# Newton step and softplus correction with one operand in PSUM, and a new placing of the stages, in a pair of Mamba scans

## The chip, the cores and the metric

The kernel runs on one core of a Trainium2 chip, as one launch that takes the whole input from HBM and leaves the whole output there. The metric is the device time of a run in microseconds (us). Three runs of the kernel before took 3250.43, 3251.8 and 3252.24 us; the median is 3251.8 us.

## The reference, cut to what matters

Four layers stand one after another on an image batch x of shape (2, 128, 56, 56), each as `x = x + layer(group_norm(x))`: an attention with agents, a 3x3 convolution, a mixture of eight experts on 2x2 patches, and a pair of Mamba blocks, one that reads each image row forwards and one that reads it backwards. The change touches the last layer alone. All of it is float32.

```python
xc = silu(conv_b + causal_conv(xi))                       # 256 channels, sequences of 56
dt, Bm, Cm = split(xc @ xproj_w.T)                        # rank 8, 16 states, 16 states
dt = softplus(dt @ dt_w.T + dt_b)
A = -exp(Alog)
for each position l:                                      # for each channel and state
    h = exp(dt_l * A) * h + (dt_l * u_l) * B_l
    y_l = sum over states (h * C_l)
y = (y + xc * D) * silu(z);  out = y @ out_w.T
...
y = concat(forward, backward) @ fuse_w.T
y = (y - mean) / sqrt(var + 1e-5) * ln_w + ln_b           # over the 128 channels
x = x + y
```

## The kernel before, in words

`mamba_pair` takes the image in 14 blocks (2 batches of 7) of 448 pixels, which are 8 image rows. Each block has two halves, f (forwards) and b (backwards), and each half has 16 units: 8 pairs of states by 2 halves of the channels. A unit is one scan over 128 partitions by 896 elements. The loop at the end of `mamba_pair` does one unit per step, so a block takes 32 steps, called f0 to f15 and b0 to b15 here, and the layer 448.

In one step the engines do this, in this order of the code. ScalarE (ACT) computes the decay exp(dt A) of the next unit (`decay`, L1648, two ACTIVATEs) into one of two PSUM tiles dA. Then ACT takes results of stages of the step before out of PSUM (`fetch`). GpSimd (POOL) computes dBu of the unit three steps ahead (`push`, L1659) into one of four buffers. VectorE (DVE) scans (`scan`, L1681). After the second scan of a pair of states, at odd units, the pair's h is multiplied by C: by POOL at L1687 for the pairs of states listed in `POOLED`, else by DVE at L1690, with C spread over the partitions by TensorE (PE) in a PSUM bank (`read_out`, L1669). PE adds up y of the unit three steps back (`collect`, L1701), and `close` (L1707, DVE) multiplies a finished y by the gate three steps into the next half.

Everything else that the blocks need is booked on steps with `book(step, stage, tag, late)` and run at the end of that step: what the next block needs before its scans (norm, convolution, silu, the low-rank product, softplus), and what the finished block needs after them (fuse, the norm over channels, turning back, adding onto x). `at` is the block's first step less 32, so that offset 0 to 31 lies in the block before and 32 to 63 in the block itself. A stage that leaves its product in PSUM returns a function that ACT runs one step later, or two with `late=1`. The order so written is the order on every engine[...]. Two single PSUM banks serve these stages: the one tagged "mm", and the one tagged "c" that `read_out` uses also. The rest of PSUM is dA (four banks) and y (two).

The two parts that the change rewrites:

The softplus of dt is log(1 + exp(-|s|)) + relu(s), with a correction. `step` (L1591) makes s on PE, and ACT writes |s| into `sp_e` and relu(s) into `dt`. `exps` (L1605) makes e = exp(-|s|) and u = 1 + e for both halves of the channels, 896 elements at a time, in SBUF. `error` (L1611, DVE) computes (u - 1) - e, what rounding added to u: two inputs, both in SBUF. `log` takes ln u, and `softplus` (L1619) adds the three terms on PE.

The norm over channels works on 112 partitions by 4 values. `measure` takes mean and variance; `root` (L1490, L1491, ACT) makes a first 1/sqrt(var + eps) through Ln and Exp into `ln_rstd` in SBUF; `newton` (L1496 to L1499, DVE) improves it by one Newton step, in three instructions with two SBUF inputs each, and makes the shift with a fourth; `normalize` (L1503, ACT) applies both.

Other names used below: `silu(inputs, gates)` (L1709) loads an activation table, does two Silu ACTIVATEs of 896 elements and loads the first table again; `weigh` (L1624, POOL) makes dt times u for `send_steps`, whose DMAs bring it to the partitions where `push` reads it; `onto` (L1524, POOL) adds the result to x.

Of the kernel before, what the change touches and what calls it, by code (L numbers as in the profile page):

```python
# [8 lines left out]
F32 = mybir.dt.float32  # L9
AF = mybir.ActivationFunctionType  # L10
ALU = mybir.AluOpType
# [6 lines left out]
P = 128  # L18
# [3 lines left out]
BLK = 448  # L22
NBLK = N // BLK
ROWS = BLK // HW
T = 112
NT = BLK // T
# [1264 lines left out]

MAMBA_STATES, MAMBA_RANK, MAMBA_TAPS = 16, 8, 4

POOLED = {"f": (0, 3, 6), "b": (1, 3)}


class MambaWeights:


    def __init__(self, net, one, nat, bank):  # L1300
# [19 lines left out]
        for n, d in enumerate("fb"):  # L1320
# [5 lines left out]
            w.d = d  # L1326
            w.pooled = POOLED[d]

# [57 lines left out]
def mamba_pair(net, out, wts, combine):  # L1386
# [5 lines left out]
    tc, nc, a = net.tc, net.nc, net.a  # L1392
# [13 lines left out]
    with ExitStack() as ctx:  # L1406
        work = ctx.enter_context(tc.tile_pool(name="l3_work", bufs=2))
# [31 lines left out]
        def mm(name):  # L1439
            return ps.tile([P, 512], F32, name=name, tag=place["tag"])  # L1440

        class Block:
# [43 lines left out]

            def root(self):
                t = net.small.tile([T, NT], F32, name="ln_t", tag="ln_t")
                self.rstd = net.small.tile([T, NT], F32, name="ln_rstd", tag="ln_rstd")
                nc.scalar.activation(t, self.mv[:, :, 1], AF.Ln, bias=net.eps[:T])  # L1490
                nc.scalar.activation(self.rstd, t, AF.Exp, scale=-0.5)  # L1491

            def newton(self):
                t = net.small.tile([T, NT], F32, name="ln_t", tag="ln_t")
                self.shift = net.small.tile([T, NT], F32, name="ln_shift", tag="ln_shift")
                nc.vector.scalar_tensor_tensor(t, self.mv[:, :, 1], 1e-5, self.rstd, ALU.add, ALU.mult)  # L1496
                nc.vector.scalar_tensor_tensor(t, t, -0.5, self.rstd, ALU.mult, ALU.mult)  # L1497
                nc.vector.scalar_tensor_tensor(self.rstd, t, 1.5, self.rstd, ALU.add, ALU.mult)  # L1498
                nc.vector.scalar_tensor_tensor(self.shift, self.mv[:, :, 0], -1.0, self.rstd, ALU.mult, ALU.mult)  # L1499

            def normalize(self):
                for t in range(NT):
# [25 lines left out]
        class Half:  # L1528
# [62 lines left out]
            def step(self, m):  # L1591
                pm = mm("dt_ps")
                nc.tensor.matmul(pm[:, :BLK], self.w.dt_t[:, m, :], self.lo[:R, :], start=True, stop=True)
                if m == 0:
                    self.e = work.tile([P, 2, BLK], F32, name="sp_e", tag="sp_e", bufs=1)
                    self.dt = work.tile([P, 2, BLK], F32, name="dt", tag="dt")
                bias = self.w.dt_b[:, m : m + 1]

                def fetch():
                    nc.scalar.activation(self.e[:, m, :], pm[:, :BLK], AF.Abs, bias=bias)  # L1600
                    nc.scalar.activation(self.dt[:, m, :], pm[:, :BLK], AF.Relu, bias=bias)

                return fetch

            def exps(self):  # L1605
                self.u = work.tile([P, 2, BLK], F32, name="sp_u", tag="sp_u", bufs=1)
                nc.scalar.activation(self.e, self.e, AF.Exp, scale=-1.0)
                nc.scalar.activation(self.u, self.e, AF.Identity, bias=1.0)

            def error(self):  # L1610
                nc.vector.scalar_tensor_tensor(self.e, self.u, 1.0, self.e, ALU.subtract, ALU.subtract)  # L1611

            def log(self):
                nc.scalar.activation(self.u, self.u, AF.Ln)  # L1614

            def softplus(self, m):
                pm = mm("sp_ps")
# [91 lines left out]
        def silu(inputs, gates):  # L1709

            if inputs:
                nc.scalar.activation(inputs.xc, inputs.xc, AF.Silu)
            if gates:
                nc.scalar.activation(gates.zs, gates.zs, AF.Silu)
            nc.scalar.preload_act_table_set(EXP_LN)  # L1715

        blocks = [Block(b, k) for b in range(NB) for k in range(NBLK)]
# [3 lines left out]
        def book(step, *stages, tag="mm", late=0):  # L1721

            agenda.setdefault(step, []).extend((stage, tag, late) for stage in stages)

        for n, blk in enumerate(blocks):

            f, b = blk.ways
            at = STEPS * (n - 1)
            if n == 0:
                book(at + 1, blk.norm)  # L1730
                for i, (h, m) in enumerate(((f, 0), (f, 1), (b, 0), (b, 1))):
                    book(at + 4 + 2 * i, lambda h=h, m=m: h.conv(m))
                    book((1, 4, 5, 13)[i], lambda h=h, m=m: h.gate(m))
                book(at + 14, lambda f=f: silu(f, None), lambda b=b: silu(b, None))
                book(at + 16, f.low)
                book(at + 17, f.send_low)
                for h, t in ((f, at + 18), (b, 2)):
                    for m in range(2):
                        book(t + m, lambda h=h, m=m: h.step(m))
                        book(t + 5 + m, lambda h=h, m=m: h.softplus(m))  # L1740
                    book(t + 2, h.exps)
                    book(t + 3, h.error)
                    book(t + 4, h.log)
                book(at + 25, f.weigh)
                book(at + 25, f.send_steps)
                book(0, b.low)
                book(2, b.send_low)
                book(11, b.weigh, b.send_steps)
            else:
                before = blocks[n - 1]  # L1750
                book(at + 4, blk.norm)
                book(at + 7, lambda f=f: f.conv(0), late=1)
                book(at + 9, lambda f=f: f.conv(1), late=1)
                book(at + 11, lambda b=b: b.conv(0), late=1)
                book(at + 11, lambda b=b: b.conv(1), tag="c", late=1)
                book(at + 12, lambda f=f, g=before.ways[0]: silu(f, g))
                book(at + 14, f.low)
                book(at + 16, lambda b=b, g=before.ways[1]: silu(b, g))
                book(at + 17, lambda f=f: f.step(0), tag="c", late=1)
                book(at + 17, lambda f=f: f.step(1), late=1)  # L1760
                book(at + 18, f.send_low)
                book(at + 20, f.exps)
                book(at + 21, f.error)
                book(at + 21, b.low, tag="c")
                book(at + 22, f.log)
                book(at + 22, lambda f=f: f.softplus(0), tag="c")
                book(at + 23, lambda f=f: f.gate(0))
                book(at + 24, lambda f=f: f.softplus(1))
                book(at + 25, lambda b=b: b.step(0), tag="c")
                book(at + 25, lambda b=b: b.step(1))  # L1770
                book(at + 26, f.weigh)
                book(at + 27, f.send_steps)
                book(at + 28, lambda f=f: f.gate(1), late=1)
                book(at + 30, b.exps)
                book(at + 30, b.error)
                book(at + 32, b.log)
                book(at + 32, lambda b=b: b.softplus(0), tag="c")
                book(at + 32, b.send_low)
                book(at + 34, lambda b=b: b.gate(0))
                book(at + 35, lambda b=b: b.softplus(1))  # L1780
                book(at + 38, b.weigh)
                book(at + 39, b.send_steps)
                book(at + 45, lambda b=b: b.gate(1))

            at = STEPS * (n + 1)
            book(at + 4, lambda blk=blk: blk.fuse(0))
            book(at + 4, lambda blk=blk: blk.fuse(1), late=1)
            book(at + 6, blk.measure)
            book(at + 9, blk.root)
            book(at + 10, blk.newton)  # L1790
            book(at + 11, blk.normalize)
            book(at + 16, blk.turn_back)
            book(at + 18, blk.onto)
        for h, step in zip(blocks[-1].ways, (12, 16)):
            book(STEPS * (len(blocks) - 1) + step, lambda h=h: silu(None, h))

        units = [(h, u) for blk in blocks for h in blk.ways for u in range(UNITS)]
# [57 lines left out]
def layers(tc, a, out, wide, attention):  # L1855
    with ExitStack() as ctx:
        net = Net(ctx, tc, a)
        keep = ctx.enter_context(tc.tile_pool(name="keep2", bufs=1, side="right"))
        with tc.tile_pool(name="l1_keep", bufs=1) as taps:
# [5 lines left out]
            with tc.tile_pool(name="l2_w", bufs=2) as wpool:  # L1865
# [62 lines left out]
```

## Time and profile before

The columns of the table are busy times in us within a window, from the trace; the borders of the windows are round numbers. The scan of the first unit starts at 1808.4 us, and the last scan ends at 3225.3 us.

| stretch | window, us | PE | DVE | ACT | POOL | PE clock |
|---|---|---|---|---|---|---|
| attention, convolution | 600 to 1000 | 381.5 | 311.1 | 241.6 | 27.2 | 0.97 |
| experts | 1000 to 1800 | 719.6 | 136.9 | 96.2 | 59.5 | 0.93 |
| one Mamba block | 2420 to 2521 | 87.8 | 96.1 | 68.9 | 93.9 | 0.90 |
| after the last scan | 3225 to 3252 | 8.5 | 5.2 | 3.5 | 1.1 | 0.75 |

How to read it: busy time on PE is that of pipelined matmuls with modelled ends, and a time on DVE counts from an instruction's start to its end, also where it stands still in between. The PE clock is what the throttle granted, as a share of full speed. The whole span is 3252.0 us.

### The profile page before, as it was taken

How to read it: one execution, taken by the hardware profiler on the slowest of the kernel's cores; microseconds unless marked ns; L12 is line 12 of the kernel's file. 1: busy time of each engine (PE TensorE's matmuls, PEld its weight loads, DVE VectorE, ACT ScalarE, POOL GpSimd, SP SyncE). 2: the span in 40 equal slices, each digit the busy share in tenths (PEclk: the TensorE clock that was granted, in tenths of full speed). 3: DMA queues.
4: the chain of work that ended last, by engine and by line, in shares of the span. 5: the costliest groups of instructions: out<-in, count | busy, mean ns of one | idle time of the engine just before them, and what ended most of it. 6: DMA issues, size and time to landing. Idle time of an engine off the chain costs nothing. (4 is left out here: it accounts for less than half of the span.)

```text
span 3252.0 us, 34415 instructions
## 1 busy us (share of the span) xinstructions
PE 2874.6 (88%) x13024; PEld 1103.7 (34%) x13024; DVE 2285.4 (70%) x1943; ACT 1738.6 (53%) x2534; POOL 1433.5 (44%) x755
## 2 busy tenths in 40 slices
PE   7899999998998899999985788988888888888885
PEld 3233333332345444444442232333323333223321
DVE  5789989998954111111113699999999999999997
ACT  5678887887801111111102567666677666776654
POOL 2000100100000100000003799898999999999995
PEclk9999999999988999999996888889899998999986
DMA  1000000000012778787753444343543435434350
GB/s 52 1 1 1 1 1 1 1 1 1 1 36 78 306 301 314 286 324 291 295 194 103 96 97 87 77 86 78 109 87 76 88 78 109 87 81 86 75 109 7
DMA packets 133397, 333.65 MB, mean 103 GB/s; under 512 B 20100, under 2 KB 90596, under 8 KB 129620
## 3 DMA queue, kind: packets, MB, share of 16 engines
q1 hardware_dynamic: 111616, 304.87, 32.7%
q0 software_dynamic: 5136, 14.70, 1.4%
q10 hardware_dynamic: 16452, 11.61, 1.1%
q8 instruction: 107, 1.75, 0.2%
q14 instruction: 86, 0.70, 0.1%
HBM read 262.56 MB, written 17.20 MB: 86 GB/s over the span
## 5 line engine op out<-in xcount | busy, mean ns | idle before, releaser
L1659 POOL TENSOR_TENSOR dBu<-dtu,Bs 128x896 f32<-128x896 f32 x448 | 944.6, 2132 | 126.1 <-DVE h L1681 77.6
L1681 DVE TENSOR_TENSOR_SCAN h<-dA,dBu 128x896 f32<-128x896 f32 x448 | 887.0, 2010 | 58.4 <-ACT dA L1648 38.1
L587 ACT ACTIVATE ex<-sc 128x896 f32<-128x896 f32 (+1 forms) x700 | 602.7, 917 | 111.6 <-PE sc L584 100.4
L594 DVE TENSOR_TENSOR ex_sum<-ex_sum,ex 128x1792 f32<-128x1792 f32 (+1 forms) x238 | 489.9, 2059 | 45.8 <-ACT ex L587 31.7
L1701 PE MATMUL y<-h,both 128*64 128x448 f32 x1792 | 470.8, 618 | 16.3 <-POOL h L1687 10.7
L584 PE MATMUL sc<-q,k 32*128 32x448 f32 (+1 forms) x2800 | 403.5, 589 | 3.6 <-ACT ex L587 2.9
L1208 PE MATMUL h_ps<-w,xs_c 128*128 128x512 f32 x896 | 392.1, 596 | 10.4 <-issue 9.9
L1648 ACT ACTIVATE dA<-dt,f_A 128x448 f32<-128x448 f32 x448 | 284.4, 637 | 170.3 <-DVE h L1681 133.3
L602 PE MATMUL av<-ex,va 128*32 128x448 f32 (+1 forms) x2800 | 335.7, 554 | 0.1
L1690 DVE TENSOR_TENSOR h<-h,c_ps 128x1792 f32<-128x1792 f32 x154 | 311.3, 2022 | 26.0 <-PE c_ps L1669 11.0
L549 POOL TENSOR_TENSOR a_e<-a_e,a_inv 112x784 f32<-112x784 f32 x14 | 41.6, 2974 | 645.5 <-ACT ex L587 436.5
L1648 ACT ACTIVATE dA<-dt,b_A 128x448 f32<-128x448 f32 x448 | 283.8, 637 | 63.3 <-DVE h L1681 55.8
L1212 DVE TENSOR_TENSOR he<-h_ps,sg 128x512 f32<-128x512 f32 x56 | 38.6, 691 | 396.9 <-PE h_ps L1208 373.7
L1159 POOL DMA_INDIRECT xr<-xd,whom x28 | 28.1, 1003 | 595.4 <-PE xr_ps L1198 492.6
L1687 POOL TENSOR_TENSOR h<-h,Cs 128x1792 f32<-128x1792 f32 x70 | 279.2, 3989 | 2.5 <-DVE h L1681 2.4
L1208 PEld LDWEIGHTS h_ps<-w,xs_c 128*128 128x128 f32 x896 | 168.6, 191 | 218.3 <-issue 201.9
L1701 PEld LDWEIGHTS y<-h,both 128*64 128x64 f32 x1792 | 118.5, 149 | 315.9 <-issue 272.8
L584 PEld LDWEIGHTS sc<-q,k 32*128 32x128 f32 (+1 forms) x2800 | 137.7, 182 | 231.2 <-issue 134.9
L1669 PE MATMUL c_ps<-low,ident 40*64 40x448 f32 x616 | 168.2, 626 | 53.7 <-DVE h L1690 34.3
L1229 PE MATMUL o_ps<-w,ht 128*128 128x512 f32 x448 | 200.2, 600 | 7.7 <-DMA w<-in_L_conv_w_dram 7.7
L1231 ACT ACTIVATE ot<-o_ps,share 128x512 f32<-128x512 f32 x28 | 19.2, 687 | 286.9 <-PE o_ps L1229 286.9
L1211 ACT ACTIVATE sg<-h_ps 128x512 f32<-128x512 f32 x56 | 33.4, 597 | 256.3 <-PE h_ps L1208 256.3
(317 smaller groups left out, 3112.0 us busy)
## 6 DMA issues: line engine op xcount, KB each, us to landing
w<-in_L_conv_w_dram SPq DMA_DIRECT2D x28, 4096.0 KB, 19.4
w<-in_L_conv_w_dram SPq DMA_DIRECT2D x28, 2048.0 KB, 10.2
Bs<-far SPq DMA_DIRECT2D x56, 896.0 KB, 10.7
dtu<-sp_u SPq DMA_DIRECT2D x112, 224.0 KB, 3.9
dt<-dt SPq DMA_DIRECT2D x112, 224.0 KB, 5.1
Cs<-far SPq DMA_DIRECT2D x140, 112.0 KB, 8.1
os<-ot ACTq DMA_DIRECT2D x28, 256.0 KB, 7.7
xd<-xt SPq DMA_DIRECT2D x14, 224.0 KB, 2.6
```

Of the source, the lines that this page charges most:

```text
L584: nc.tensor.matmul(sc[:size, j, :BLK], self.m.k[rows, at : at + size], self.q[rows, :], start=True, stop=True)
L587: nc.scalar.activation(ex[:size, 2 * g : 2 * g + 2, :], sc[:size, :, :BLK], AF.Exp, scale=scale)
L594: nc.vector.tensor_add(self.total[g][:size], self.total[g][:size], ex[:size])
L602: nc.tensor.matmul(self.av[rows, :BLK], self.m.va[:size, i, rows], self.ex[i][:size, h, :], start=i == 0, stop=i == STEPS - 1,)
L1208: nc.tensor.matmul(h_ps, xc[:, q, :], w1[:, q, f0 : f0 + 512], start=q == 0, stop=q == 3)
L1229: nc.tensor.matmul(o_ps, ht[:, i, :], w2[:, i, :], start=i == 0, stop=i == nj - 1)
L1648: nc.scalar.activation(self.dA[u][:, r * BLK : (r + 1) * BLK], self.dt2[:, m, r, :], AF.Exp, scale=self.w.A[:, j, 2 * m + r : 2 * m + r + 1],)
L1659: nc.gpsimd.tensor_tensor(self.dBu[u], self.dtu2[:, m], self.B[:, j, :].unsqueeze(1).to_broadcast(shape), ALU.mult)
L1681: nc.vector.tensor_tensor_scan(hf, af, bf, 0.0, ALU.mult, ALU.add)
L1687: nc.gpsimd.tensor_tensor(h4, h4, c, ALU.mult)
L1690: nc.vector.tensor_tensor(h4, h4, c, ALU.mult)
L1701: nc.tensor.matmul(self.y[r * H : (r + 1) * H, m, :BLK], both, self.hc[j][:, m, r, :], start=False, stop=j == PAIRS - 1)
```

## The change

It has three parts.

First, `root` leaves its result in a PSUM bank (`ln_ps`, the "c" bank) instead of SBUF. `newton` then has one of its two inputs in PSUM in each instruction, writes the improved root into PSUM, and a fifth instruction copies it to SBUF for `normalize`.

Second, 1 + e stays in the PSUM bank where s was: ACT writes it over s, half of the channels at a time. `exps` goes into the fetch of `step`, and `error` and `log` are done per half of 448 elements, with u read from PSUM. The bank "mm" is held from the product of `step` until `log` has read it.

Third, most stages are booked on other steps, and of the b half the pairs of states 0 and 3, not 1 and 3, are multiplied by POOL. The purpose is to have no DVE instruction with both inputs in SBUF in these two places, and to place the stages so that banks and engines are free for the new order.

```diff
-POOLED = {"f": (0, 3, 6), "b": (1, 3)}
+POOLED = {"f": (0, 3, 6), "b": (0, 3)}
...
             def root(self):
                 t = net.small.tile([T, NT], F32, name="ln_t", tag="ln_t")
+                self.rs = mm("ln_ps")[:T]
+                nc.scalar.activation(t, self.mv[:, :, 1], AF.Ln, bias=net.eps[:T])
+                nc.scalar.activation(self.rs[:, :NT], t, AF.Exp, scale=-0.5)
...
-                nc.vector.scalar_tensor_tensor(t, self.mv[:, :, 1], 1e-5, self.rstd, ALU.add, ALU.mult)
-                nc.vector.scalar_tensor_tensor(t, t, -0.5, self.rstd, ALU.mult, ALU.mult)
-                nc.vector.scalar_tensor_tensor(self.rstd, t, 1.5, self.rstd, ALU.add, ALU.mult)
-                nc.vector.scalar_tensor_tensor(self.shift, self.mv[:, :, 0], -1.0, self.rstd, ALU.mult, ALU.mult)
+                nc.vector.scalar_tensor_tensor(t, self.mv[:, :, 1], 1e-5, r, ALU.add, ALU.mult)
+                nc.vector.scalar_tensor_tensor(t, t, -0.5, r, ALU.mult, ALU.mult)
+                nc.vector.scalar_tensor_tensor(r, t, 1.5, r, ALU.add, ALU.mult)
+                nc.vector.tensor_copy(self.rstd, r)
+                nc.vector.scalar_tensor_tensor(self.shift, self.mv[:, :, 0], -1.0, r, ALU.mult, ALU.mult)
...
                 def fetch():
-                    nc.scalar.activation(self.e[:, m, :], pm[:, :BLK], AF.Abs, bias=bias)
+                    e = self.e[:, m, :]
+                    nc.scalar.activation(e, pm[:, :BLK], AF.Abs, bias=bias)
                     nc.scalar.activation(self.dt[:, m, :], pm[:, :BLK], AF.Relu, bias=bias)
+                    nc.scalar.activation(e, e, AF.Exp, scale=-1.0)
+                    nc.scalar.activation(pm[:, :BLK], e, AF.Identity, bias=1.0)
...
-            def exps(self):
-                self.u = work.tile([P, 2, BLK], F32, name="sp_u", tag="sp_u", bufs=1)
-                nc.scalar.activation(self.e, self.e, AF.Exp, scale=-1.0)
-                nc.scalar.activation(self.u, self.e, AF.Identity, bias=1.0)
-            def error(self):
-                nc.vector.scalar_tensor_tensor(self.e, self.u, 1.0, self.e, ALU.subtract, ALU.subtract)
-            def log(self):
-                nc.scalar.activation(self.u, self.u, AF.Ln)
+            def error(self, m):
+                e = self.e[:, m, :]
+                nc.vector.scalar_tensor_tensor(e, self.ue[m], 1.0, e, ALU.subtract, ALU.subtract)
+            def log(self, m):
+                if m == 0:
+                    self.u = work.tile([P, 2, BLK], F32, name="sp_u", tag="sp_u", bufs=1)
+                nc.scalar.activation(self.u[:, m, :], self.ue[m], AF.Ln)
...
-                book(at + 12, lambda f=f, g=before.ways[0]: silu(f, g))
-                book(at + 14, f.low)
-                book(at + 16, lambda b=b, g=before.ways[1]: silu(b, g))
+                book(at + 10, lambda f=f, g=before.ways[0]: silu(f, g))
+                book(at + 12, lambda b=b: b.conv(0))
+                book(at + 12, lambda b=b: b.conv(1), tag="c", late=1)
+                book(at + 15, f.low, tag="c")
+                book(at + 17, f.send_low)
+                book(at + 17, lambda f=f: f.step(0))
+                book(at + 18, lambda b=b, g=before.ways[1]: silu(b, g))
+                book(at + 19, lambda f=f: f.error(0))
+                book(at + 19, lambda f=f: f.log(0))
+                book(at + 20, lambda f=f: f.step(1))
+                book(at + 21, lambda f=f: f.error(1))
+                book(at + 22, lambda f=f: f.log(1))
...
-                book(at + 26, f.weigh)
+                book(at + 25, f.weigh)
...
+                book(at + 27, lambda b=b: b.step(0))
+                book(at + 28, lambda b=b: b.error(0))
+                book(at + 28, lambda b=b: b.log(0))
+                book(at + 29, lambda b=b: b.step(1))
+                book(at + 31, lambda b=b: b.error(1))
+                book(at + 31, lambda b=b: b.log(1))
...
-            book(at + 9, blk.root)
-            book(at + 10, blk.newton)
-            book(at + 11, blk.normalize)
+            book(at + 7, blk.root, tag="c", late=1)
+            book(at + 7, blk.newton)
+            book(at + 15, blk.normalize)
             book(at + 16, blk.turn_back)
-            book(at + 18, blk.onto)
+            book(at + 31, blk.onto)
```

More of the change, by code (lines that the diff above doesn't have):

```diff
@@ L1488, in root, with newton @@
                 t = net.small.tile([T, NT], F32, name="ln_t", tag="ln_t")
+                self.rs = mm("ln_ps")[:T]
+                nc.scalar.activation(t, self.mv[:, :, 1], AF.Ln, bias=net.eps[:T])
+                nc.scalar.activation(self.rs[:, :NT], t, AF.Exp, scale=-0.5)
+            def newton(self):
+                r = self.rs[:, :NT]
+                t = net.small.tile([T, NT], F32, name="ln_t", tag="ln_t")
                 self.rstd = net.small.tile([T, NT], F32, name="ln_rstd", tag="ln_rstd")
[L1490 to L1494, printed above, removed]
                 self.shift = net.small.tile([T, NT], F32, name="ln_shift", tag="ln_shift")
[L1496 to L1499, printed above, removed]
+                nc.vector.scalar_tensor_tensor(t, self.mv[:, :, 1], 1e-5, r, ALU.add, ALU.mult)
[3 more added lines that the diff above has]
+                nc.vector.scalar_tensor_tensor(self.shift, self.mv[:, :, 0], -1.0, r, ALU.mult, ALU.mult)
             def normalize(self):
@@ L1596, in step @@
                     self.dt = work.tile([P, 2, BLK], F32, name="dt", tag="dt")
+                    self.ue = {}
+                self.ue[m] = pm[:, :BLK]
                 bias = self.w.dt_b[:, m : m + 1]
                 def fetch():
-                    nc.scalar.activation(self.e[:, m, :], pm[:, :BLK], AF.Abs, bias=bias)
+                    e = self.e[:, m, :]
+                    nc.scalar.activation(e, pm[:, :BLK], AF.Abs, bias=bias)
                     nc.scalar.activation(self.dt[:, m, :], pm[:, :BLK], AF.Relu, bias=bias)
-                return fetch
-            def exps(self):
-                self.u = work.tile([P, 2, BLK], F32, name="sp_u", tag="sp_u", bufs=1)
-                nc.scalar.activation(self.e, self.e, AF.Exp, scale=-1.0)
-                nc.scalar.activation(self.u, self.e, AF.Identity, bias=1.0)
-            def error(self):
-                nc.vector.scalar_tensor_tensor(self.e, self.u, 1.0, self.e, ALU.subtract, ALU.subtract)
-            def log(self):
-                nc.scalar.activation(self.u, self.u, AF.Ln)
+                    nc.scalar.activation(e, e, AF.Exp, scale=-1.0)
+                    nc.scalar.activation(pm[:, :BLK], e, AF.Identity, bias=1.0)
+                return fetch
+            def error(self, m):
[5 more added lines that the diff above has]
+                nc.scalar.activation(self.u[:, m, :], self.ue[m], AF.Ln)
             def softplus(self, m):
@@ L1736, in mamba_pair @@
                 book(at + 17, f.send_low)
-                for h, t in ((f, at + 18), (b, 2)):
+                for h, t in ((f, at + 16), (b, 0)):
                     for m in range(2):
[L1739 to L1743, printed above, removed]
+                        book(t + 2 + 3 * m, lambda h=h, m=m: h.step(m))
+                        book(t + 3 + 3 * m, lambda h=h, m=m: h.error(m))
+                        book(t + 4 + 3 * m, lambda h=h, m=m: h.log(m))
+                        book(t + 7 + m, lambda h=h, m=m: h.softplus(m))
                 book(at + 25, f.weigh)
@@ L1750, in mamba_pair @@
                 before = blocks[n - 1]
[L1751 to L1755, printed above, removed]
-                book(at + 12, lambda f=f, g=before.ways[0]: silu(f, g))
-                book(at + 14, f.low)
-                book(at + 16, lambda b=b, g=before.ways[1]: silu(b, g))
@@ L1759, in mamba_pair @@
[L1759 to L1765, printed above, removed]
+                book(at + 6, blk.norm)
+                book(at + 7, lambda f=f: f.conv(0))
+                book(at + 8, lambda f=f: f.conv(1), late=1)
+                book(at + 10, lambda f=f, g=before.ways[0]: silu(f, g))
@@ L1766, in mamba_pair @@
+                book(at + 21, lambda f=f: f.error(1))
+                book(at + 22, lambda f=f: f.log(1))
                 book(at + 22, lambda f=f: f.softplus(0), tag="c")
-                book(at + 23, lambda f=f: f.gate(0))
+                book(at + 23, b.low)
                 book(at + 24, lambda f=f: f.softplus(1))
-                book(at + 25, lambda b=b: b.step(0), tag="c")
-                book(at + 25, lambda b=b: b.step(1))
-                book(at + 26, f.weigh)
+                book(at + 25, f.weigh)
@@ L1772, in mamba_pair @@
+                book(at + 26, lambda f=f: f.gate(0))
+                book(at + 27, lambda b=b: b.step(0))
                 book(at + 27, f.send_steps)
[L1773 to L1776, printed above, removed]
+                book(at + 28, lambda b=b: b.error(0))
+                book(at + 28, lambda b=b: b.log(0))
+                book(at + 29, lambda b=b: b.step(1))
+                book(at + 31, lambda b=b: b.error(1))
@@ L1777, in mamba_pair @@
+                book(at + 31, lambda b=b: b.log(1))
                 book(at + 32, lambda b=b: b.softplus(0), tag="c")
-                book(at + 32, b.send_low)
-                book(at + 34, lambda b=b: b.gate(0))
-                book(at + 35, lambda b=b: b.softplus(1))
+                book(at + 33, lambda f=f: f.gate(1), late=1)
+                book(at + 33, lambda b=b: b.softplus(1), tag="c")
+                book(at + 33, b.send_low)
+                book(at + 35, lambda b=b: b.gate(0))
@@ L1781, in mamba_pair @@
                 book(at + 38, b.weigh)
-                book(at + 39, b.send_steps)
-                book(at + 45, lambda b=b: b.gate(1))
+                book(at + 43, b.send_steps)
+                book(at + 46, lambda b=b: b.gate(1), late=1)
             at = STEPS * (n + 1)
@@ L1788, in mamba_pair @@
             book(at + 6, blk.measure)
-            book(at + 9, blk.root)
-            book(at + 10, blk.newton)
-            book(at + 11, blk.normalize)
+            book(at + 7, blk.root, tag="c", late=1)
+            book(at + 7, blk.newton)
+            book(at + 15, blk.normalize)
             book(at + 16, blk.turn_back)
-            book(at + 18, blk.onto)
-        for h, step in zip(blocks[-1].ways, (12, 16)):
+            book(at + 31, blk.onto)
+        for h, step in zip(blocks[-1].ways, (10, 18)):
             book(STEPS * (len(blocks) - 1) + step, lambda h=h: silu(None, h))
```

## The prediction, made before the run

> **What bounds the kernel now.** I read the busy times by window first, to find the stretch that the change touches. Two neighbouring Mamba blocks, busy us and counts in the order PE, PEld, DVE, ACT, POOL, then the PE clock:
>
> ```profile
> 2420.00:2521.00 101.00, 87.79 (x298) 30.92 (x300) 96.13 (x60) 68.86 (x110) 93.89 (x43) 0.90 0.44 91
> 2521.00:2621.00 100.00, 82.28 (x296) 29.52 (x292) 96.02 (x60) 68.42 (x110) 90.89 (x43) 0.93 0.41 85
> ```
>
> DVE is busy 96 of 101 us, POOL 91 to 94, PE 82 to 88, ACT 69. So DVE sets the pace, with POOL close behind and PE not far. The scans run from 1808.4 to 3225.3 us: 1416.9 us for 448 steps, 101.2 us per block of 32 (100.7 in the steady blocks).
>
> Next, what DVE's busy time consists of. The groups of instructions by tile and line give durations (min/median/max, ns):
>
> ```profile
> L1496 DVE SCALAR_TENSOR_TENSOR ln_t<-ln_mv,ln_rstd x14: 161/379/650, 1947.2 to 3236.2; 112x4 f32<-112x4 f32 x14
> L1497 DVE SCALAR_TENSOR_TENSOR ln_t<-ln_t,ln_rstd x14: 163/2009/2016, 1947.8 to 3236.4; 112x4 f32<-112x4 f32 x14
> L1498 DVE SCALAR_TENSOR_TENSOR ln_rstd<-ln_t,ln_rstd x14: 161/1999/2006, 1949.8 to 3236.6; 112x4 f32<-112x4 f32 x14
> ...
> L1611 DVE SCALAR_TENSOR_TENSOR sp_e<-sp_u,sp_e x28: 1090/2297/4700, 1784.2 to 3125.9; 128x896 f32<-128x896 f32 x28
> ...
> L1707 DVE TENSOR_TENSOR yv<-y,zs x28: 1064/1083/1092, 1874.3 to 3229.3; 128x896 f32<-128x896 f32 x28
> ```
>
> Four elements per partition take 2.0 us, where the smallest time of the same instruction is 0.16 us. The timeline of one Newton step shows why (start us, length us):
>
> ```profile
> 2456.53 0.53 DVE L1496 SCALAR_TENSOR_TENSOR ln_t<-ln_mv,ln_rstd 112x4 f32<-112x4 f32 x1
> 2457.09 2.00 DVE L1497 SCALAR_TENSOR_TENSOR ln_t<-ln_t,ln_rstd 112x4 f32<-112x4 f32 x1
> 2459.13 2.00 DVE L1498 SCALAR_TENSOR_TENSOR ln_rstd<-ln_t,ln_rstd 112x4 f32<-112x4 f32 x1
> 2461.16 0.16 DVE L1499 SCALAR_TENSOR_TENSOR ln_shift<-ln_mv,ln_rstd 112x4 f32<-112x4 f32 x1
> ...
> 2452.91 8.20 POOL L1659 TENSOR_TENSOR dBu<-dtu,Bs 128x896 f32<-128x896 f32 x4
> 2463.34 2.09 POOL L1659 TENSOR_TENSOR dBu<-dtu,Bs 128x896 f32<-128x896 f32 x1 [2.24 <-DVE h L1681]
> ```
>
> POOL does four dBu of 2.05 us each, and DVE's tiny instructions each end with one of them; L1499 runs free once POOL has run out of buffers. After the last scan, when POOL is idle, the four start at 3236.18, 3236.37, 3236.57 and 3236.77 us and take 0.16 to 0.17 us. L1611 is the same case: 2.3 us, against 1.08 us for L1707, which has as many elements and one input in PSUM. The wait goes both ways:
>
> ```profile
> 2393.47 7.12 POOL L1659 TENSOR_TENSOR dBu<-dtu,Bs 128x896 f32<-128x896 f32 x3
> ...
> 2404.52 6.17 POOL L1659 TENSOR_TENSOR dBu<-dtu,Bs 128x896 f32<-128x896 f32 x3
> ```
>
> The first three dBu lie around an L1611, the second three do not: POOL loses about 0.9 us to each L1611.
>
> **What the Trainium skill says.** "SBUF — State Buffer", section "SBUF: two separate sides": the port pair shared by GpSimd and VectorE is an exclusive lock, taken by a VectorE instruction with two SBUF inputs against a GpSimd one that reads SBUF; whoever starts first has it for the whole instruction. The trace agrees: 2.00 us for four elements. It also shows the way out: the scan L1681 (dA in PSUM) and L1690 (c_ps in PSUM) run at 2.01 and 2.02 us with POOL busy beside them. "VectorE: DVE Perf Modes", section "The TRN2 errata — SBUF-src ops pay a fixed extra latency per instruction", prices a PSUM source at (120 + elements)/0.96 ns: 1058 ns for 896, where L1707 shows 1083; by it an instruction of 448 takes 592 ns, an estimate. "ScalarE: Activation LUTs", section "What ACT_TABLE_LOAD costs", gives 1283 ns for a table load, and L1712 shows exactly this.
>
> **The change part by part.** Steps count from the starts of the scans. Gaps between starts: a scan 1.93 us, L1690 2.11, L1707 1.02, the measure 1.05. A block's DVE sum before: 32 x 1.93 + 11 x 2.11 + 2 x 1.02 + 1.05 = 88.1; Newton 4.65 (step f10 lasts 6.56 against 1.93); two L1611 at 1.95 and 2.19, 4.15. Total 96.9, and 3.7 of idle before scans (for ACT's dA, POOL's dBu, c_ps) make 100.6.
>
> Newton: five instructions spaced 0.20 us as in the tail, 1.0 us instead of 4.65. Bounds: 0.8 (four) to 1.4 us (five with a longer PSUM access, up to 0.28 as for a small ACT instruction on ln_t). I take 1.0; it saves 3.65.
>
> Softplus correction: four instructions of 448 instead of two of 896. From L1707, 1.02 less 448/0.96 ns gives 0.55 each, 2.1 us in all (bounds 1.9 to 2.4) instead of 4.15. It saves 2.05.
>
> DVE's sum becomes 88.1 + 1.0 + 2.1 = 91.2 us.
>
> POOL: 32 x 2.05 + 5 x 3.98 + 2 x 2.2 (`weigh`) + 1.1 (`onto`) = 91.0, and before 1.7 more beside L1611. Its idle time before was 8.4 us: 5.8 for free buffers, that is for DVE, and 2.6 for the DMA of dtu at f0. `weigh` of f one step earlier puts one more dBu of 2.05 us ahead of that wait, so most of it goes. The exchange of pair 1 for 0 costs no engine anything; it frees bank "c" from f15 to b2, where `low` now goes.
>
> ACT: per half of a block Exp, Identity and Ln go from three of 0.95 to six of about 0.57 (0.19 fixed, half the elements): +0.55, 1.1 us per block on 69. It lies in ACT's idle time, but it stands in queues that matter, so I went through them. The deadline is that the decay of step k+1 ends before its scan.
> - silu at f10: ACT has the fetch of conv(1), which PE finishes late because conv(0) and `read_out` of f8 precede it, then 4.45 us of silu (2 x 1.28 + 0.95 + 0.93), then the decay for f12: about 0.9 us too late.
> - silu at b2: before it now stand a decay (1.27) and the whole fetch of `step` (2 x 0.63 + 2 x 0.56 = 2.4), after it the decay for b4. Counted from b2's start with ACT 0.4 us behind: 0.4 + 1.3 + 2.4 + 4.45 + 1.3 = 9.8 us. DVE wants it after b2 and b3 (1.93 + scan, L1690, L1707, error: 5.6) at 7.5. 2.3 us late. Before, silu stood at b0, and DVE waited 0.1 before b2.
> - `log` at b12 and b15 waits on ACT for `error` of the same step; behind it stands the next decay. By the same count it ends 2.1 us before its scan at b12, and 0.15 late at b15.
> - `newton` in the step of `root`: the root is done 0.8 us after the scan of f7 starts, 1.1 us before DVE asks. `read_out` of f8 waits for the bank, and its product is wanted a step later. No cost.
> With 0.4 for c_ps and dBu the idle time comes to 3.7 us: what it was. So the two queues of silu take the place of the waits for dA, dBu and dtu removed, and the block falls by the DVE savings alone, 5.7 us, to 94.9.
>
> PE: 82 to 88 us busy and some 15 idle, of which 4 are the wait of `softplus` at f0 for ln u (now booked one step after `log`). In 95 us it still fits. [...]the four blocks from 2010 to 2320 us at 0.84 to 0.87 took 103 to 104 us, those at 0.90 to 0.93 100 to 101. I give back 0.4 us per block.
>
> Sum: 13 Newton steps lie beside POOL: 13 x 3.65 = 47.5. Of 28 L1611, 27: 27 x 1.03 = 27.8. Less 14 x 0.4 = 5.6 for the clock: 69.7. 3251.8 - 70 = 3182 us.
>
> **The rivals.** (1) The new queues cost nothing, and POOL and DVE, 91.0 and 91.2, set the end with about 1.2 of coupling: 92.4 per block, 8.3 x 13.5 less: 3140 us. For it: both silu lie where f10 and b3 leave room; against it: the count at b2. (2) PE or ACT become the bound for part of a block: bank "mm" is held by u for three steps, four times per block[...]. If this takes 2.6 us more per block, 35 more: 3217 us. For it: PE's 88 of 101 us, and ACT waits of up to 2.5 us for sp_ps, 1.8 for fuse_ps; against it: of these waits none reached DVE. (3) Slower: silu at b2 hits an ACT already late (PE brings `low` and z after bank "c" is freed at the end of f15), 4.5 instead of 2.3; conv at f10 2 instead of 0.9; each `log` behind `error` 1.5 at two steps: 6.3 per block, 85 us: 3267. Against it: ACT has 32 of 101 us idle, and an ACT that is late catches up at each L1690.
>
> **How the numbers follow.** The forecast 0.6, (1) 0.15, (2) 0.16, (3) 0.09. The range runs from rival (1) to beyond rival (2), 3138 to 3228, and leaves out (3) and part of (1). The savings' own bounds (Newton 3.25 to 3.85, correction 1.75 to 2.25, so 9 us in all) lie within it. Faster 0.9, no change 0.02 (it needs waits of 5.5 us), slower 0.08.
>
> **What would show it.** Right: Newton's instructions at 0.15 to 0.3 us in mid-stretch, the corrections at about 0.6, POOL's dBu at 2.05 without the long ones, a block of about 95 us, a DVE wait for dA of about 2 us before b4, DVE and POOL both at 95%. Wrong: instructions with a PSUM input that still last until POOL's end; waits of DVE for dA or c_ps over 6 us per block; a PE clock under 0.85.

## The result, and the profile after

The changed kernel takes 3175.82 us (median of four runs, 3174.22 to 3176.32) where the kernel before, beside it, takes 3252.02 us: a ratio of 0.9761, with a 95% interval from 0.9744 to 0.9778. Later, on another occasion, it gave 0.9769 (0.9748 to 0.9791). The forecast was 3182 us.

The spans of the two profiles, 3252.0 and 3173.7 us, differ by 78.3 us. The scans run from 1808.0 to 3146.0 us now, 1338.0 us instead of 1416.9: the whole difference lies in the loop over the 448 steps. In the blocks 4 to 12 the period falls from 101.1 to 95.6 us.

The busy times in a window of the Mamba loop of the changed kernel (columns as before: PE, PEld, DVE, ACT, POOL, PE clock, DMA share, GB/s):

```profile
2400.00:2501.00 101.00, 92.99 (x317) 31.72 (x314) 95.67 (x66) 72.92 (x121) 97.22 (x46) 0.90 0.48 98
```

The window of 101 us now holds more than one block, since a block takes 95.6 us. DVE is at 95%, as before, but POOL at 96% and PE at 92% have come up to it: three engines are within a few per cent of each other.

The instructions that were changed, in the groups by tile (duration min/median/max, ns):

```profile
L1499 DVE SCALAR_TENSOR_TENSOR ln_t<-ln_mv,ln_ps x14: 129/132/158, 1936.2 to 3157.8; 112x4 f32<-112x4 f32 x14
L1500 DVE SCALAR_TENSOR_TENSOR ln_t<-ln_t,ln_ps x14: 157/158/159, 1936.3 to 3158.0; 112x4 f32<-112x4 f32 x14
L1501 DVE SCALAR_TENSOR_TENSOR ln_ps<-ln_t,ln_ps x14: 166/166/168, 1936.5 to 3158.2; 112x4 f32<-112x4 f32 x14
...
L1617 DVE SCALAR_TENSOR_TENSOR sp_e<-dt_ps,sp_e x56: 599/618/626, 1779.2 to 3058.4; 128x448 f32<-128x448 f32 x56
```

The 2.0 us are gone, in every one of the 14 blocks: maximum and minimum lie within 30 ns, whatever POOL does beside it. The pages have the two large groups of POOL and DVE (busy us, mean ns, then idle before and its releaser), first of the kernel before, then of the changed one:

```profile
L1659 POOL TENSOR_TENSOR dBu<-dtu,Bs 128x896 f32<-128x896 f32 x448 | 944.6, 2132 | 126.1 <-DVE h L1681 77.6
L1681 DVE TENSOR_TENSOR_SCAN h<-dA,dBu 128x896 f32<-128x896 f32 x448 | 887.0, 2010 | 58.4 <-ACT dA L1648 38.1
...
L1667 POOL TENSOR_TENSOR dBu<-dtu,Bs 128x896 f32<-128x896 f32 x448 | 923.2, 2087 | 72.2 <-DVE h L1689 52.2
L1689 DVE TENSOR_TENSOR_SCAN h<-dA,dBu 128x896 f32<-128x896 f32 x448 | 878.6, 2006 | 58.1 <-ACT dA L1656 56.5
```

The mean dBu fell from 2132 to 2087 ns, so POOL's losses beside the old correction are gone as well, and its idle time went from 126.1 to 72.2 us. DVE's idle time before scans is what it was, 58.1 after 58.4 us, and 56.5 of it are decays that ACT brings late. For the kernel before, the list of waits (us in total, times, longest) names two causes:

```profile
DVE h L1681 <- ACT dA L1648: 38.1, 44, 9.2
DVE h L1681 <- POOL dBu L1659: 18.7, 21, 1.2
```

The second is misleading. A scan needs both its decay and its dBu, and 20 of its 21 waits, 17.6 of the 18.7 us, end 0.09 to 0.10 us after the end of the scan's decay, while its dBu was done at least 5 us before: 9.3 us before in the 12 waits of 1.18 us at f14. So late decays are nearly the whole of this idle time before the change as well as after it.

The waits of DVE in two blocks (2303 to 2494 us) of the changed kernel come from the list of who waited for whom (us in total, times, longest):

```profile
DVE h L1689 <- ACT dA L1656: 7.3, 7, 2.0
```

The longest is the one before b4 that the prediction counted out. DVE's timeline there, with the start, the length and in brackets the idle time before:

```profile
2350.89 0.61 DVE L1617 SCALAR_TENSOR_TENSOR sp_e<-dt_ps,sp_e 128x448 f32<-128x448 f32 x1
2353.48 3.94 DVE L1689 TENSOR_TENSOR_SCAN h<-dA,dBu 128x896 f32<-128x896 f32 x2 [1.98 <-ACT dA L1656]
2357.52 2.02 DVE L1698 TENSOR_TENSOR h<-h,c_ps 128x1792 f32<-128x1792 f32 x1
2360.59 0.62 DVE L1617 SCALAR_TENSOR_TENSOR sp_e<-dt_ps,sp_e 128x448 f32<-128x448 f32 x1 [1.05 <-ACT dt_ps L1611]
```

And ACT's queue at the same place one block later:

```profile
2441.04 1.30 ACT L1656 ACTIVATE dA<-dt,b_A 128x448 f32<-128x448 f32 x2
2442.28 0.61 ACT L1607 ACTIVATE sp_e<-dt_ps,c_L_conv_f_dt_b 128x448 f32<-128x448 f32 x1
...
2443.91 0.55 ACT L1611 ACTIVATE dt_ps<-sp_e 128x448 f32<-128x448 f32 x1
2444.48 1.28 ACT L1720 ACT_TABLE_LOAD   x1
...
2447.58 1.28 ACT L1723 ACT_TABLE_LOAD   x1
2448.87 1.31 ACT L1656 ACTIVATE dA<-dt,b_A 128x448 f32<-128x448 f32 x2
```

A decay, the fetch of `step`, silu and the next decay stand one behind another without a gap from 2441.04 to 2450.18 us, 9.1 us, while DVE has 7.5 us of work.

### The profile page after: what moved, and what is told of

Read it like the earlier page. It is cut to its first block, busy times and chain, and to the rows that moved or that the text cites. A ratio compares the mean times of both kernels' runs of the same rounds, so it can differ in the third digit from the quotient of the medians.

```text
span 3173.7 us, 34586 instructions
## 1 busy us (share of the span) xinstructions
PE 2863.2 (90%) x13024; PEld 1091.1 (34%) x13024; DVE 2201.9 (69%) x1985; ACT 1752.3 (55%) x2618; POOL 1411.1 (44%) x755
## 5 line engine op out<-in xcount | busy, mean ns | idle before, releaser
L1667 POOL TENSOR_TENSOR dBu<-dtu,Bs 128x896 f32<-128x896 f32 x448 | 923.2, 2087 | 72.2 <-DVE h L1689 52.2
L1689 DVE TENSOR_TENSOR_SCAN h<-dA,dBu 128x896 f32<-128x896 f32 x448 | 878.6, 2006 | 58.1 <-ACT dA L1656 56.5
```

The lines of the kernel that those rows point to most:

```text
L1667: nc.gpsimd.tensor_tensor(self.dBu[u], self.dtu2[:, m], self.B[:, j, :].unsqueeze(1).to_broadcast(shape), ALU.mult)
L1689: nc.vector.tensor_tensor_scan(hf, af, bf, 0.0, ALU.mult, ALU.add)
```

## The experiments

Runs of one group shared one chip and the runs of the kernel before on it, which were between 3250 and 3258 us in median; ratios to those are compared, not times. The labels e1, e2 and so on stand for the runs. Waits are means over the blocks 4 to 12, read off the starts of the scans and the idle times in each trace.

**Newton alone (e1).** Theory: both inputs in SBUF make DVE wait for POOL. Rival: the new placing brings the gain.

```diff
 # kernel before; root and newton as in the change
-            book(at + 9, blk.root)
-            book(at + 10, blk.newton)
+            book(at + 7, blk.root, tag="c")
+            book(at + 7, blk.newton)
```

> The kernel before with the Newton part of the change alone: root and newton at step f7 with the root in bank c, all else as before. If DVE stands still in the Newton step because both inputs lie in SBUF while POOL reads SBUF, its four instructions fall from 4.65 us to five at 0.13 to 0.2 us, 1.0 us in all, and 13 blocks give 13 x 3.65 = 47 us: 3205 us. If the gain of the change comes from the new placing of the stages, or if the 2.0 us are a wait that moves on to the next scan, nothing changes: 3245 to 3252 us.

Measured: 3220.88 us, ratio 0.9899 (0.9882 to 0.9915), 29 us. The Newton step itself does what was expected: 4.63 us at f10 become 0.68 at f7. But the period falls by 2.5 us only. DVE's and ACT's timelines of e1 show where the rest went:

```profile
2451.12 3.93 DVE L1685 TENSOR_TENSOR_SCAN h<-dA,dBu 128x896 f32<-128x896 f32 x2
2457.60 2.02 DVE L1685 TENSOR_TENSOR_SCAN h<-dA,dBu 128x896 f32<-128x896 f32 x1 [2.55 <-issue]
...
2447.20 1.31 ACT L1652 ACTIVATE dA<-dt,f_A 128x448 f32<-128x448 f32 x2 [2.75 <-DVE h L1685]
...
2448.96 1.64 ACT L1507 ACTIVATE ln_y<-ln_y,ln_shift,ln_rstd 112x128 f32<-112x128 f32 x4
...
2451.81 1.28 ACT L1716 ACT_TABLE_LOAD   x1
...
2454.91 1.28 ACT L1719 ACT_TABLE_LOAD   x1
2456.20 1.31 ACT L1652 ACTIVATE dA<-dt,f_A 128x448 f32<-128x448 f32 x2
```

The scan of f14 starts 0.09 us after the decay behind silu ends. The same place in the kernel before:

```profile
2456.64 1.31 ACT L1648 ACTIVATE dA<-dt,f_A 128x448 f32<-128x448 f32 x2 [2.49 <-DVE h L1681]
...
2461.36 1.65 ACT L1503 ACTIVATE ln_y<-ln_y,ln_shift,ln_rstd 112x128 f32<-112x128 f32 x4 [2.86 <-DVE ln_shift L1499]
...
2464.62 1.28 ACT L1712 ACT_TABLE_LOAD   x1
...
2469.02 1.31 ACT L1648 ACTIVATE dA<-dt,f_A 128x448 f32<-128x448 f32 x2
...
2470.42 2.02 DVE L1681 TENSOR_TENSOR_SCAN h<-dA,dBu 128x896 f32<-128x896 f32 x1 [1.18 <-POOL dBu L1659]
```

There too the scan of f14 starts 0.09 us after the decay behind silu ends (2470.33 us), so the wait of 1.18 us was one for ACT, though the profile names POOL. While DVE stood in the Newton step, from 2456.53 to 2461.32 us, ACT got through the decay of f12 and the fetch of a convolution, and then itself waited 2.86 us for Newton's last result before `normalize`. In e1 all of these stand in silu's queue while DVE goes on, and the wait grows from 1.18 to 2.55 us. These 1.4 us of the 3.95 us that Newton saves are lost, which leaves the 2.5.

**Back to SBUF, one part at a time, in the changed kernel (e2, e3, e4).** The first undoes the Newton part (the old `root` and `newton` at the new steps), the second the correction (u in an SBUF tile that is free at that time), the third both.

```diff
 # second of the three
-                    nc.scalar.activation(pm[:, :BLK], e, AF.Identity, bias=1.0)
+                    nc.scalar.activation(self.ue[:, m, :], e, AF.Identity, bias=1.0)   # ue: SBUF
```

> The changed kernel with the root and the Newton step back in SBUF, at the new steps. If both inputs in SBUF are the cause, two or three of the four instructions last 2 us again and the time rises by up to 47 us, to 3215 to 3223 us. If the placing is the cause, 3176 to 3182 us.

> The changed kernel with u = 1 + e written to a tile of its own in SBUF, so that the four corrections of 448 elements per block have both inputs in SBUF; steps and banks as in the changed kernel, though bank mm is free earlier. If DVE waits for a POOL instruction that is under way, each correction takes 0.55 us plus about half to one and a half POOL instructions' rest, 1 us on average: 4 us per block, 54 us in all: 3230 us. If an input in SBUF merely costs another fixed access time, the corrections stay at 0.55 to 0.65 us and the time at 3172 to 3180 us.

> The changed kernel with both parts back in SBUF: what is left is the new placing, the halved corrections and the pairs of states that POOL multiplies. If the two waits for POOL are the whole gain and add up, 3176 + 47 + 54 = 3277 us, slower than before. If the placing brings part of the gain, below 3245 us.

Measured: 3254.29 us, ratio 1.0013 (1.0000 to 1.0026); 3210.98 us, 0.9878 (0.9858 to 0.9899); 3283.19 us, 1.0091 (1.0074 to 1.0109). All three go the way of the theory, none has the expected size: 78 us instead of 47 for Newton, 35 instead of 54 for the correction.

Newton's excess is the cleanest evidence for the cause. At f7 POOL has not a dBu under way but the long product of a pair of states. The timelines of DVE and POOL with Newton in SBUF:

```profile
2551.06 0.81 DVE L1496 SCALAR_TENSOR_TENSOR ln_t<-ln_mv,ln_rstd 112x4 f32<-112x4 f32 x1
2551.90 3.91 DVE L1497 SCALAR_TENSOR_TENSOR ln_t<-ln_t,ln_rstd 112x4 f32<-112x4 f32 x1
2555.84 2.00 DVE L1498 SCALAR_TENSOR_TENSOR ln_rstd<-ln_t,ln_rstd 112x4 f32<-112x4 f32 x1
...
2549.77 2.08 POOL L1663 TENSOR_TENSOR dBu<-dtu,Bs 128x896 f32<-128x896 f32 x1
2551.81 3.98 POOL L1691 TENSOR_TENSOR h<-h,Cs 128x1792 f32<-128x1792 f32 x1
2555.75 2.07 POOL L1663 TENSOR_TENSOR dBu<-dtu,Bs 128x896 f32<-128x896 f32 x1
```

The same instruction on four elements that took 2.00 us in the kernel before takes 3.91 us beside a POOL instruction of 3.98 us. It lasts as long as what POOL is doing, whatever that is; a fixed access cost can't do this. Step f7 lasts 8.65 us against 2.61 in the changed kernel; about 0.9 come back because the wait before f12 is hidden in it, and the period rises by 5.5 us.

The corrections do wait in SBUF (min/median/max, ns):

```profile
L1616 DVE SCALAR_TENSOR_TENSOR sp_e<-sp_w,sp_e x56: 616/1839/6264, 1779.7 to 3092.5; 128x448 f32<-128x448 f32 x56
```

In the mean over the blocks 4 to 12 that makes the four corrections of a block 5.2 us longer, but the period rises by 2.8 us only: the one at b3 lies in the shadow of ACT's queue, whose wait before b4 shrinks from 1.98 to 0.39 us, and DVE's other waits shrink by 0.7 us together. Why these shrink was not tried.

With both in SBUF the kernel is 0.9% slower than the kernel before. The new placing and the halved corrections alone are a loss, then: they pay only with the operands in PSUM. A large part of that loss may be where Newton now stands: beside the long POOL product its instructions last 6.8 us per block, against 4.6 at f10 in the kernel before, which over 13 blocks makes an estimated 29 us, where the whole loss is 33.

**The b half's silu (e6, then e10).** The prediction put 2.3 us of DVE's wait down to silu at b2.

```diff
-                nc.scalar.activation(inputs.xc, inputs.xc, AF.Silu)
+                nc.scalar.activation(inputs.xc, inputs.xc, kind)      # Identity for b
...
-            nc.scalar.preload_act_table_set(EXP_LN)
+            if not light:
+                nc.scalar.preload_act_table_set(EXP_LN)
```

> The changed kernel with Identity in place of the Silu of the b half and without its two table loads, so that the b half's silu is left out of the computation and 2.57 us leave ACT's queue at b2. If that queue is what holds DVE before b4 (1.98 us) and b5's correction (0.47 us), both vanish: 13 x 2.4 = 31 us: 3144 us. If POOL sets the pace once DVE no longer waits, at 91.0 us of work and some 2.5 us of waiting that can't be avoided, 25 us or less: 3150 to 3165 us. If the wait has another cause, 3174 us.

Measured: 3182.03 us, ratio 0.9767 (0.9750 to 0.9783): no gain at all. The wait before b4 is gone, and DVE waits elsewhere. DVE, PE and ACT without the b half's silu:

```profile
2462.37 0.62 DVE L1617 SCALAR_TENSOR_TENSOR sp_e<-dt_ps,sp_e 128x448 f32<-128x448 f32 x1
2462.90 4.04 DVE L1689 TENSOR_TENSOR_SCAN h<-dA,dBu 128x896 f32<-128x896 f32 x2
2467.05 2.02 DVE L1698 TENSOR_TENSOR h<-h,c_ps 128x1792 f32<-128x1792 f32 x1
2471.55 0.62 DVE L1617 SCALAR_TENSOR_TENSOR sp_e<-dt_ps,sp_e 128x448 f32<-128x448 f32 x1 [2.48 <-ACT dt_ps L1611]
...
2463.00 3.35 PE L1705 MATMUL y<-xc,b_skip 128*128 128x448 f32 x4
2466.28 1.76 PE L1709 MATMUL y<-h,both 128*64 128x448 f32 x4
2467.97 1.29 PE L1597 MATMUL dt_ps<-low,f_dt_t 8*128 8x448 f32 x2
...
2469.30 0.64 ACT L1607 ACTIVATE sp_e<-dt_ps,c_L_conv_f_dt_b 128x448 f32<-128x448 f32 x1 [3.04 <-PE dt_ps L1597]
```

The b half's y starts on PE once `close` has read the f half's (at 2462.4), and the second product of `step` stands behind it; ACT waits 3.04 us for that product, and the correction at b5 waits for ACT. This chain is there in the changed kernel too, right behind ACT's queue: in the blocks 4 to 12 ACT waits 0.5 to 1.7 us for the same product, and DVE 0.47 us in the mean before the correction. To test it, the correction was moved one step on, to b6, where its log stood already, with silu still left out:

```diff
-                book(at + 21, lambda f=f: f.error(1))
+                book(at + 22, lambda f=f: f.error(1))
                 book(at + 22, lambda f=f: f.log(1))
```

> The kernel of e6 (the b half's silu left out, Identity in its place) with the f half's second correction and its log one step later, at b6. In e6 the wait before b4 is gone and DVE waits 2.22 us at b5 for the second half's u instead: ACT gets the product of step late, because on PE it stands behind the first matmuls of y of the b half, which wait for close at b3. If that PE queue is a second limit right behind ACT's, and the correction's place is all that makes it reach DVE, both waits are gone now: 13 x 2.2 = 29 us less than e6: 0.967 of the kernel before. If POOL holds the pace, 0.973 to 0.977, as e6.

Measured: 3157.91 us, ratio 0.9720 (0.9697 to 0.9743), where the changed kernel beside it gave 0.9769 and e6 0.9767: 16 us less, half of what was expected. The wait before the correction falls to 0.33 us, but 0.47 each appear before b7 and b9. So the two chains, ACT's and PE's, hold DVE at nearly the same time: to take ACT's away alone brought nothing. To move the correction alone, with silu in place, was not tried. POOL was not the next limit: in e10 it is still idle for 3.2 us per block.

**Versions that keep silu (e5, e7, e9; e12 is the changed kernel again).** The first gives ln u a tile of its own, the second moves silu and the first log, the third moves the second correction, and norm and the f half's convolutions, too. In code, the second:

```diff
-                book(at + 18, lambda b=b, g=before.ways[1]: silu(b, g))
-                book(at + 19, lambda f=f: f.log(0))
+                book(at + 19, lambda b=b, g=before.ways[1]: silu(b, g))
+                book(at + 20, lambda f=f: f.log(0))
```

> The changed kernel with ln u in a tile that is free at that time, instead of the tile from which the DMAs of dtu read: log of the b half no longer waits on ACT for the DMAs of the f half (3.4 us per block at b12 in the changed kernel). If this ACT wait reaches DVE only as the 0.44 us before b14, 13 x 0.44 = 6 us: 3170 us. If POOL, which is then as busy as DVE, sets the pace, no change: 3174 to 3176 us.

> The kernel of e5 with the b half's silu one step later, at b3 and ahead of the log of the f half, which goes to b4. By the count of ACT's queue the decay for b4 is then in time and the one for b5 1.6 us late, instead of 1.98 + 0.47: 0.8 us per block, 11 us: 3159 us. If the queue only moves its delay, 3170 us; if log, now later, delays the second product of step and the correction behind it, above 3175 us.

> The changed kernel with three moves: ln u in its own tile (e5), the b half's silu at b3 and the first log at b4 (e7), the f half's second correction and log at b6, and from the third block on norm and the f half's convolutions one step earlier. Of e7's waits the 0.82 us at b5 and the 0.84 us before f12 should go: 13 x 1.66 = 22 us against e7: 0.969. If the queues merely shift, 0.974 to 0.977; if POOL holds the pace, the same.

> The changed kernel once more, beside e9 and e10 on their chip: 0.976 of the kernel before.

Measured: 0.9755 (0.9739 to 0.9772), 0.9758 (0.9739 to 0.9778), and 0.9807 (0.9784 to 0.9829) for the third, with 0.9769 for the changed kernel beside it. In the profiles the loop falls by 2 and 6 us in the first two, which the interval doesn't tell from nothing; in e7 the 1.98 us before b4 turn into 1.30 us for the decay before b5 and 0.82 us before the correction that follows. (In five of the nine blocks the profile puts the 1.30 us down to POOL, but the decay ends 0.10 us before the scan in all of them, and the unit's dBu 2.1 us before.) In the third the wait before f12 vanishes as meant, and a new one of 2.30 us stands before the Newton step: on ACT `root` now stands behind the fetch of a convolution that PE brings 2.8 us late. None beats the changed kernel clearly.

**Newton alone, with silu at its new step (e8).** The f half's convolutions come one step earlier too, as in the change.

```diff
 # e1
-                book(at + 12, lambda f=f, g=before.ways[0]: silu(f, g))
+                book(at + 10, lambda f=f, g=before.ways[0]: silu(f, g))
```

> The Newton part alone (as e1) and the f half's convolutions and silu two steps earlier, as in the change. In e1 DVE waits 2.55 us before f14 for a decay that stands behind silu on ACT, instead of 1.18 for POOL before. If that is where the missing 18 us of e1 went, the earlier silu gives most of it back: 3203 us. If the 18 us went elsewhere, 3221 us.

Measured: 3236.21 us, ratio 0.9941 (0.9925 to 0.9957), slower than e1. The 2.55 us before f14 vanish, but 1.55 and 0.75 us stand before f12 and f13: here `normalize`, still at f11, is behind silu and ahead of the decays of f13 and f14 (ACT: silu from 2444.69, `normalize` from 2450.34, the decays from 2451.88 us), and the waits at f3 and b3 grow from 0.55 and 0.13 us to 1 us each. The change moves `normalize` to f15 too.

**The exchange of pairs (e13).**

```diff
-POOLED = {"f": (0, 3, 6), "b": (0, 3)}
+POOLED = {"f": (0, 3, 6), "b": (1, 3)}
```

> The changed kernel with the b half's pairs of states 1 and 3 on POOL, as before the change. Bank c is then wanted by read_out at b0, where low holds it until ACT's copy 2.3 us after b0 starts: c_ps would be there 3.3 us after it, and L1698 asks 3.9 us after it. If the exchange costs no engine anything, as I predicted, the queue of silu gives 2.4 us at b4 instead of 1.98, 5 us in all: 0.977 to 0.979 of the kernel before. If the bank becomes a wait of its own (c_ps before b1, and z and dt_ps behind it on PE), 1 us or more per block: 0.981 or above.

Measured: 3187.97 us, ratio 0.9804 (0.9790 to 0.9818). Between the two expectations; no wait for c_ps appears at b1, but the one before b4 is 3.35 us instead of 1.98. The DVE product of 2.1 us then lies at b1, ahead of silu's queue, where it helps no one; at b3 it covers part of that queue. By the ratios the exchange is worth some 11 us, but the intervals of the two kernels touch (0.9790 and 0.9791), and the period of the blocks 4 to 12 differs by 0.4 us only.

## Why the prediction held, point by point

- **Cause.** DVE's long small instructions are waits for POOL, and an operand in PSUM ends them. Shown: by e2 (2.00 us become 3.91 beside a longer POOL instruction), e1 and e3, and by the changed profile.
- **Newton, 4.65 to 1.0 us.** Measured 0.68 us (f7 lasts 2.61, a bare scan 1.93), below the lower bound of 0.8 that I gave. It saves 3.95 us instead of 3.65.
- **Correction, 0.55 us each.** Measured 0.52 us at b12, and 0.5 to 0.6 at the other three steps. DVE's sum of 91.2 us per block is 95.6 less 4.5 of idle time, 91.1.
- **Queues.** Expected 2.3 us at b4, 0.9 before f12, 0.15 at b15, 0.4 for the rest: 3.7. Measured 1.98 before b4 and 0.47 at b5, 0.83 before f12, 0.44 before b14, 0.45 for c_ps at f3, 0.33 elsewhere: 4.5, where the kernel before had 3.7. So the waits did not stay what they were, they grew by 0.8 us per block. I missed that `log` of b, now earlier, has to wait on ACT for the DMAs that still read the tile (3.4 us per block, 0.44 of it reach DVE at b14). And I counted the wait before f14 in the kernel before among those for dBu. It was silu's queue on ACT, then at f12, as the timelines beside e1 show: the change moved this queue more than it put a new one in the place of another wait.
- **DMA of dtu.** POOL's wait fell from 2.6 to 0.3 us, as expected of the earlier `weigh`.
- **Clock.** I gave 0.4 us per block back for a lower clock. It did not come: over the blocks the clock was 0.90 before and 0.91 after, with PE busy for 91% of the time instead of 86%. This step failed. The blocks that I took it from, from 2010 to 2320 us, are three and not four, and each holds 296 matmuls like the ones around it: at the lower clock the same work took longer, and that more work lowers the clock can't be read from them. In the changed kernel the same three blocks have 0.91 to 0.93 and take 94.6 to 96.3 us instead of 102.3 to 103.8, some 7 us more gained than the other steady blocks give. Why the clock was lower there before stays open.
- **The sum.** It came out near by luck in part. In the blocks 6 to 13 the period falls from 100.7 to 95.5 us, by 5.2, where the forecast had 5.7 less 0.4. The waits that grew by 0.8 us were not in it; Newton's 0.3 us more and the clock's 0.4 us that did not come make up for most of them. What lies between 3182 and 3176 us is about what the three blocks named above gained more.
- **"The exchange costs no engine anything."** It seems to gain a little: with the old pairs the wait before b4 is 1.37 us longer (e13), and the period of the blocks 4 to 12 is longer by 0.4 us.
- **The parts' savings as a sum.** 47.5 and 27.8 us fit the whole change only. Alone, Newton brings 29 (e1); taken away, it costs 78 (e2). A saving on DVE counts only as far as ACT's queue at the same place lets it. These queues are the reason why the stages had to be placed anew.
- **Rivals.** The first (queues cost nothing) fell with the waits measured, and POOL's limit was not reached: even in e10, the fastest run, POOL is idle for 3.2 us per block. The second was right in kind: PE's chain through `close` and `step` is a second limit (e6, e10), though in the changed kernel it cost DVE no more than the 0.47 us at b5.

## What to carry to other kernels

When a tiny VectorE instruction lasts as long as a GpSimd one beside it, it is waiting, not working: the profile books this as busy time. So look at the least duration of the group (0.16 us here, where the median was 2.0) and try one of its two SBUF inputs in PSUM. When VectorE is the pace-setter, time taken out at one step shows the queues of other engines that it had hidden; count them (what stands before the next needed result, in order, against the work that covers it) and place the stages again. Before removing a wait, ask what would end just after it: here two chains ended within half a microsecond, and removing the first gave nothing. And where a wait has two inputs, compare the ends of both with its end before you believe the engine that the profile names: at f14 it named POOL, but the wait was for ACT.

## What the runs showed that was not expected

- A row of VectorE instructions with two SBUF inputs loses its turn each time: in e2 one of them gets through per POOL instruction, and POOL's next one starts first (2551.81 before 2551.90, 2555.75 before 2555.84 us above). Two tiny instructions in a row cost two whole POOL instructions, 5.9 us. It can be worse. In e3 one correction of 448 elements started while a dBu was under way and sat through it and the two after it, which ended at 2760.00 us:

```profile
2754.22 6.26 DVE L1616 SCALAR_TENSOR_TENSOR sp_e<-sp_w,sp_e 128x448 f32<-128x448 f32 x1
...
2753.82 6.18 POOL L1666 TENSOR_TENSOR dBu<-dtu,Bs 128x896 f32<-128x896 f32 x3
```

What decides how many turns are lost was not tried.

- `log` on ACT starts right after `error` on DVE (2463.07 after 2462.99 us in e6), though it needs nothing that `error` writes. Both read the same PSUM bank. Whether this is why it waits was not tried.
